# Seven 128-wide block products in place of a two-by-two block product of eight, in a graph network of four layers on one Trainium2 core

## The chip, the core and the metric

The kernel runs on one NeuronCore of a Trainium2 chip. A core has TensorE for matrix products (PE in the profile, with its weight loads in a row of their own, PEld), VectorE (DVE), ScalarE (ACT), GpSimd (POOL) and SyncE (SP), which here only starts DMA transfers. The metric is the device time of one execution in microseconds. Before the change it is 1382.38 us, the median of three runs (1381.41 to 1382.77).

## What is computed

The input `x` has 64 batches of 256 nodes with 128 features, all in fp32, and one 256x256 matrix `adj`, called A here, is shared by all batches. Four layers follow each other, and each ends with a residual sum and a layer norm (LN). Cut to what matters:

```python
def _layernorm(x, axis=-1, eps=1e-5):
    m = jnp.mean(x, axis=axis, keepdims=True)
    v = jnp.var(x, axis=axis, keepdims=True)
    return (x - m) / jnp.sqrt(v + eps)
# layer 0: powers of A up to the third
parts = [x_1[..., None], _chebyshev(adj0, x_1, CONV_ORDER), _chebyshev(adj1, x_1, CONV_ORDER)]
y_1 = jnp.einsum('bnik,iok->bno', jnp.concatenate(parts, axis=3), weight_1)
# layer 1
output = jnp.einsum('nm,bmo->bno', adj, jnp.einsum('bnf,fo->bno', x, weight)) + bias
# layer 2, A_norm = d (A + I) d
out = jnp.einsum('bnc,oc->bno', jnp.einsum('nm,bmc->bnc', A_norm, x), W) + b
# layer 3: five steps of a gated unit, both matrices are A
m_in = jnp.einsum('nm,bmd->bnd', in_matrix, h)
u3 = h @ u3_w.T + u3_b
z = jax.nn.sigmoid(av @ w3_w.T + w3_b + u3)
r = jax.nn.sigmoid(av @ w4_w.T + w4_b + u3)
hv = jnp.tanh(av @ w5_w.T + w5_b + (r * h @ u5_w.T + u5_b))
h = (1.0 - z) * h + z * hv
```

Every one of the 64 batches is therefore multiplied by A, by A squared or by the normalised A eight times in the form that the kernel uses: once in layer 0 (with A squared; the rest of layer 0 is folded into products with the weights and one more product with A), once in layer 1, once in layer 2 and five times in layer 3.

## The kernel before

**Tiling.** The batches are taken in groups of two (`NB`), so that a group's activations fill one tile of 128 partitions by 512 fp32 numbers: two batches times two halves of the nodes times 128 features. There are 31 groups of two and, because `ONES` is (0, 2), two groups of one batch at the end. A product with A (`propagate`, L457) takes each batch's two halves of the nodes as stationary operands of 128x128 and streams the 256 columns of A's transpose past each, four matmuls per group into one PSUM bank, and ScalarE copies the bank to SBUF (`copied`, L417). Each matmul instruction of the program appears twice in the trace[...]: counts of matmuls in the profile are twice those of the program.

**What else a group does.** Layer 0 has 8 matmuls of 256 columns with the weights and 4 of 256 columns with A; layers 1 and 2 have 4 matmuls each of 128 columns with the weights; each step of layer 3 has five matmuls of 512 columns (`product`, L517) in transposed form, three activations on ScalarE (`gate_`, L520: r, z, hv) and four elementwise operations on VectorE (`tensor`, L527: rh, d, e, hT), and then a transpose of 32x32 blocks on VectorE and a way through DRAM that brings h back with the nodes on the partitions (`packed`, L500). The last step of a group goes back through DRAM too (`turned`, `brought`), or, for the last `END` batches, through TensorE.

**LN.** `statistics` (L422) takes four `bn_stats` and four `bn_aggr` on VectorE, adds the epsilon there, and raises to the power of -1/2 on GpSimd (`rs`). `normalise` (L446) then subtracts the mean and multiplies by `rs` on VectorE, in four instructions of 128 columns. In layers 1 and 2 GpSimd also adds the bias to the residual (`yb`, L595).

**The order of the work.** Nothing is left to a scheduler at run time. Each operation is entered in a `Plan` (L50) with its engine, a cost in ns, a lag until others can see its result and a rank. `Plan.order` (L80) then plays the program through: of all operations whose inputs are there it takes the one that can start first, and among those that can start together the one of the lowest rank, that is of the oldest group.

```python
                    key = (max(at, t0), op.rank, op.seq)
                    if pick is None or key < pick[0]:
                        pick = (key, op)
```

The operations are issued in the order of their planned starts, and each engine runs its own in that order. The plan's costs are `pe_cost`, `dve_cost` and `act_cost` (L141 to L149) or numbers written at the call. The plan also gives out buffers: eight PSUM banks, 54 tiles of the kind `w`, and so on (`slots`, L199).

**Groups in flight.** A group may begin only when the group `ACTIVE` places before it has finished (`gate`, L649 to L653), so at most six groups are under way. The last `LEVEL` groups get nearly equal ranks, which lets them advance side by side to the end.

Of the kernel before, what the change touches and what calls it, by code (L numbers as in the profile page):

```python
# [13 lines left out]
P = 128  # L14
NB = 2
ACTIVE = 6
HEAD = 4
LEVEL = 6
END = 8
STEPS = 5  # L20
WARM = 12
ONES = (0, 2)
# [4 lines left out]
class Val:  # L27
# [3 lines left out]
    def __init__(self, kind, shape, name, nb=NB):  # L31
        self.kind, self.shape, self.name, self.nb = kind, shape, name, nb
        self.writer, self.readers, self.users = None, [], []
        self.slot = self.tile = None
# [15 lines left out]
class Plan:  # L50
# [9 lines left out]
    def add(self, engine, cost, lag, rank, run, reads=(), writes=(), after=()):  # L60
        if engine == "SP":
            lag += 700
        op = Op(len(self.ops), rank, engine, cost, lag, run, [*reads, *writes])
        op.deps.update(after)
        for v in reads:
            op.deps.add(v.writer)
            v.readers.append(op)
        for v in writes:
            if v.writer is not None:
                op.deps.add(v.writer)  # L70
            op.deps.update(v.readers)
            v.writer, v.readers = op, []
# [72 lines left out]
def dve_cost(elements):  # L145
    return elements / 0.96 + 75
# [7 lines left out]
def kernel(  # L154
# [42 lines left out]
    SHAPES = {"bank": [P, 512], "x": [P, 512], "w": [P, 512], "st": [P, Q * 6], "mv": [P, Q * 2],  # L197
              "ve": [P, Q], "rs": [P, Q]}
    slots = {"bank": BANKS, "x": ACTIVE + 3, "w": 54, "dram1": 8, "dram2": 16, "st": 8, "mv": 8, "ve": 8, "rs": 8}  # L199
# [15 lines left out]
    def load(rank, name, shape, src):  # L215
        v = constant(name, shape)
# [13 lines left out]
    def warmed():  # L230
        for i in range(WARM):
# [5 lines left out]
    a_nat = load(-9, "a_nat", [P, T, N], adj.rearrange("(t p) m -> p t m", p=P))  # L237
# [12 lines left out]
    pre(-8, "PE", 4 * 110, lambda: turn(p_at, a_nat), [a_nat], [p_at])  # L250
# [42 lines left out]
    ahat, anT = constant("ahat", [P, T, N]), constant("anT", [P, T, N])  # L293
# [24 lines left out]


    w1s = load(1.3, "w1s", [P, C], w1)  # L320
    b1s = load(1.4, "b1s", [P, C], bass.AP(tensor=b1.tensor, offset=b1.offset, ap=[[0, P], [1, C]]))
    raw = {name: load(1.5, f"raw_{name}", [P, src.shape[1]], src)
           for name, src in (("w2", w2), ("w4", w4_w), ("w3", w3_w), ("w5", w5_w), ("u3", u3_w), ("u5", u5_w))}
    b2s = load(1.5, "b2s", [P, C], bass.AP(tensor=b2.tensor, offset=b2.offset, ap=[[0, P], [1, C]]))
    both = {name: constant(f"both_{name}", [P, C]) for name in ("w4", "w3", "w5", "w34")}
# [41 lines left out]
    def tile_of(v, q):  # L367
        return nat(v)[:, q, :]

    def pair_of(v, q):  # L370
        return v.ap.rearrange("p (b c t) -> p b t c", c=C, t=T)[:, q // T, q % T, :]
# [8 lines left out]
    class Group:  # L380
# [15 lines left out]
        def rank(self):  # L396
            g = self.start / NB
            return g if g < G - LEVEL else G - LEVEL + (g - G + LEVEL) / 10 + self.count / 100

        def add(self, engine, cost, lag, run, reads=(), writes=()):  # L400
            after = () if self.first else self.gate
            self.count += 1
            op = plan.add(engine, cost, lag, self.rank(), run, reads, writes, after)
# [296 lines left out]
```

## Time and profile before

The page of the profile says of one execution:

| | busy, us | share of 1380.7 us | instructions |
|---|---|---|---|
| PE | 1366.5 | 99% | 5044 |
| PE weight loads | 922.5 | 67% | 5044 |
| DVE | 970.5 | 70% | 2735 |
| ACT | 513.1 | 37% | 833 |
| POOL | 236.1 | 17% | 205 |

Busy time is the time in which an engine had at least one instruction under way. A matmul's duration is longer than its distance to the next one[...]; so a matmul's price is read from the distance between starts in the timeline, not from the mean duration in a group. In a line of the groups, the numbers are: the line of the source, the engine, the operation, what is written and what is read, the shape, the count, the busy time in us, the mean duration of one in ns, and the idle time of the engine just before them. A line of the timeline has the start in us, the length of the (merged) piece in us, then the same names.

### The profile page before, as it was taken

To read this page: it belongs to the slowest core of one execution; us is meant where nothing else is said; L and a number is where in the kernel's file an instruction comes from. 1 tells how busy PE (TensorE), PEld (TensorE's weight loads), DVE (VectorE), ACT (ScalarE), POOL (GpSimd) and SP (SyncE) were. 2 spreads that over 40 slices of the span, in tenths; PEclk is the share of its full clock that TensorE was granted. 3 is DMA by queue.
4 is the path that set the end of the run, shared out by engine and by line. 5 is a ranking of instruction groups with operands and counts; after the bars stand their busy time and mean duration, and the time that the engine had idled before them with its cause. 6 is when DMAs were issued, how large, how long until landed. Compare 5 with 4: busy or idle time off the path is not lost.

```text
span 1380.7 us, 16602 instructions
## 1 busy us (share of the span) xinstructions
PE 1366.5 (99%) x5044; PEld 922.5 (67%) x5044; DVE 970.5 (70%) x2735; ACT 513.1 (37%) x833; POOL 236.1 (17%) x205
## 2 busy tenths in 40 slices
PE   9999999999999999999999999999999999999996
PEld 8866666666667766566676666667666677766664
DVE  4755686867667767776686767668685778875577
ACT  2233433333433233433424333442334332334443
POOL 1400021202111211011121211012221113210001
PEclk9999999999999999999999999999999999999999
DMA  6023233333333332343241334333232432233332
GB/s 177 31 77 91 85 115 115 91 98 105 112 107 90 109 92 75 97 137 110 64 137 54 108 108 117 95 92 106 78 107 84 118 97 85 85 92 90 86 103 65
DMA packets 271112, 134.08 MB, mean 97 GB/s; under 512 B 177584, under 2 KB 243632, under 8 KB 271024
## 3 DMA queue, kind: packets, MB, share of 16 engines
q1 hardware_dynamic: 271024, 133.03, 33.2%
q8 instruction: 40, 0.66, 0.2%
q14 instruction: 48, 0.39, 0.1%
HBM read 67.05 MB, written 65.54 MB: 96 GB/s over the span
## 4 chain that ended last, share of the span: by engine, by line
PE 97%; DVE 2%; DMA 0%; ACT 0%; issue 0%; POOL 0%; SPq 0%; POOLq 0%; DVEq 0%
PE pr L195 30%; PE ph L195 19%; PE pmg L195 19%; PE py L195 16%; PE pm L195 8%; PE pmq L195 4%; DVE y L451 1%; DMA h<-dh 0%; DVE st L427 0%; PE p_a L195 0%; PE warm L232 0%; DVE s L443 0%; DVE d L529 0%; DVE mv L431 0%; DVE e L529 0%
## 5 line engine op out<-in xcount | busy, mean ns | idle before, releaser
L195 PE MATMUL pr<-mg,w435u5T 128*128 128x512 f32 (+1 forms) x660 | 323.3, 580 | 1.7 <-ACT mg L419 1.4
L438 POOL TENSOR_TENSOR rs<-ve,half 128x4 f32<-128x4 f32 (+1 forms) x132 | 137.9, 1049 | 1049.8 <-DVE ve L432 1049.7
L529 DVE TENSOR_TENSOR d<-hv,hT 128x512 f32<-128x512 f32 (+1 forms) x165 | 113.6, 690 | 189.6 <-ACT hv L522 189.2
L195 PE MATMUL pmg<-aTp,h 128*128 128x256 f32 x1024 | 241.7, 379 | 0.4 <-DMA h<-dh 0.4
L195 PEld LDWEIGHTS pmg<-aTp,h 128*128 128x128 f32 x1024 | 200.4, 196 | 50.5 <-issue 24.4
L529 DVE TENSOR_TENSOR rh<-r,hT 128x512 f32<-128x512 f32 (+1 forms) x165 | 116.5, 706 | 128.2 <-ACT r L522 126.9
L195 PEld LDWEIGHTS pr<-mg,w435u5T 128*128 128x128 f32 x660 | 123.6, 190 | 101.0 <-issue 90.4
L419 ACT COPY mg<-pmg 128x512 f32<-128x512 f32 (+1 forms) x165 | 94.6, 573 | 257.0 <-PE pmg L195 236.5
L451 DVE TENSOR_SCALAR y<-s,mv,rs 128x128 f32<-128x128 f32 x512 | 149.7, 357 | 34.0 <-POOL rs L438 32.5
L195 PE MATMUL pr<-hT,w2u3T 128*128 128x512 f32 (+1 forms) x330 | 163.1, 580 | 1.1 <-DVE hT L529 1.1
L522 ACT ACTIVATE z<-pr,bsum 128x512 f32<-128x512 f32 (+1 forms) x165 | 111.3, 674 | 142.2 <-PE pr L195 137.4
L195 PE MATMUL ph<-mg,w435u5T 128*128 128x512 f32 (+1 forms) x330 | 163.4, 579 | 0.0
L195 PE MATMUL ph<-rh,w435u5T 128*128 128x512 f32 (+1 forms) x330 | 163.0, 579 | 0.0
L522 ACT ACTIVATE r<-pr,bsum 128x512 f32<-128x512 f32 (+1 forms) x165 | 111.3, 674 | 135.2 <-PE pr L195 132.7
L522 ACT ACTIVATE hv<-ph,bsum 128x512 f32<-128x512 f32 (+1 forms) x165 | 111.3, 674 | 53.0 <-PE ph L195 50.9
L529 DVE TENSOR_TENSOR e<-z,d 128x512 f32<-128x512 f32 (+1 forms) x165 | 113.8, 691 | 2.5
L529 DVE TENSOR_TENSOR hT<-hT,e 128x512 f32<-128x512 f32 (+1 forms) x165 | 113.1, 687 | 2.5
L427 DVE BATCH_NORM_STATS2 st<-s 128x6 f32<-128x128 f32 x512 | 109.7, 277 | 0.8
L195 PEld LDWEIGHTS ph<-rh,w435u5T 128*128 128x128 f32 x330 | 62.4, 190 | 69.3 <-issue 59.5
L195 PEld LDWEIGHTS ph<-mg,w435u5T 128*128 128x128 f32 x330 | 62.4, 190 | 67.5 <-issue 54.8
L504 DVE STREAM_TRANSPOSE th<-hT 128x512 f32<-128x512 f32 x132 | 91.0, 689 | 2.0
L195 PEld LDWEIGHTS pr<-hT,w2u3T 128*128 128x128 f32 x330 | 61.6, 190 | 42.0 <-issue 25.2
(79 smaller groups left out, 1373.7 us busy)
## 6 DMA issues: line engine op xcount, KB each, us to landing
dh<-th SPq DMA_DIRECT2D x155, 256.0 KB, 2.0
h<-dh SPq DMA_DIRECT2D x256, 128.0 KB, 2.5
x<-in_x_dram SPq DMA_DIRECT2D x31, 256.0 KB, 3.3
hT<-dh SPq DMA_DIRECT2D x124, 64.0 KB, 2.0
out_dram<-y SPq DMA_DIRECT2D x31, 256.0 KB, 2.4
xT<-dx SPq DMA_DIRECT2D x60, 128.0 KB, 2.5
dx<-tx SPq DMA_DIRECT2D x29, 256.0 KB, 2.6
dn<-tn SPq DMA_DIRECT2D x28, 256.0 KB, 2.0
```

The source lines that it names most:

```text
L195: nc.tensor.matmul(o, lhsT, rhs, start=start, stop=stop, skip_group_check=shared)
L419: self.act(lambda: nc.scalar.copy(t.ap, ps.ap), [ps], [t])
L427: nc.vector.bn_stats(st.ap[:, q * 6:(q + 1) * 6], nat(s)[:, q, :])
L438: lambda: nc.gpsimd.tensor_tensor(rs.ap, ve.ap, half[:, :self.q], op=OP.pow), [ve], [rs])
L451: nc.vector.tensor_scalar(nat(y)[:, q, :], nat(s)[:, q, :], mv.ap[:, 2 * q:2 * q + 1], rs.ap[:, q:q + 1], op0=OP.subtract, op1=OP.mult)
L504: self.dve(lambda: nc.vector.transpose(turn.ap.rearrange("p (u j t) -> p u t j", t=T, j=32), src.ap.rearrange("p (u t i) -> p u t i", t=T, ...
L522: self.act(lambda: nc.scalar.activation(t.ap, ps.ap, func, bias=bias[1], scale=1.0), [ps, bias[0]], [t], act_cost(self.width) + 100)
L529: self.dve(lambda: nc.vector.tensor_tensor(out(t), way(a), way(b), op=op), [a, b], [t])
```

## The change

The matrix A is cut into four blocks of 128x128, and the activations of a group into two batches and two halves of nodes. That is a product of two-by-two blocks, which takes eight block products; the change uses a scheme of the Strassen and Winograd kind that needs seven, at the price of sums and differences of blocks before and after. For groups of two batches `propagate` now hands over to a new method, `seven`:

- The sums of A's blocks are made once at the start (`block_sums`), for A, A squared, the normalised A and a row-permuted A.
- The differences of the activations' blocks are made on GpSimd, in three instructions per product with A: `ts01` (256 columns), `ts2` and `ts3` (128 columns each).
- The seven products have 128 columns each and come in four pieces: `first` (one product), `middle` (three), `more` (one) and `rest` (two). All four write one PSUM bank. ScalarE saves the result of `first` before `more` adds to it (`kept`).
- The sums afterwards are four instructions on VectorE (`post11`, `post12`, `post13` of 128 columns and `post2` of 256) and one copy of 128 columns on ScalarE. They take the place of the copy of 512 columns on ScalarE. `rest` has to wait for `post13` and for that copy[...].

The other parts: the last step of LN moves from VectorE to ScalarE (`activation` with scale and bias per partition), for which VectorE negates the mean and GpSimd multiplies it by `rs`; the copies of layer 0's sums out of PSUM move from VectorE to ScalarE; at most eight groups are in flight instead of six, with more buffers of several kinds; there are 32 groups of two batches and none of one; `LEVEL` is 5 instead of 6 and the ranks of the last groups rise faster; the plan's cost of a VectorE operation is raised by 6%, and the new operations have costs written at the call; a few more transposes are made at the start[...]. Some tiles of the preparation are now given out by the plan and reused. The first two groups keep the old four matmuls in layer 0.

```diff
@@ -13,13 +13,13 @@
-ACTIVE = 6
+ACTIVE = 8
 HEAD = 4
-LEVEL = 6
+LEVEL = 5
 END = 8
 STEPS = 5
-WARM = 12
-ONES = (0, 2)
+WARM = 14
+ONES = (0, 0)
...
-    def add(self, engine, cost, lag, rank, run, reads=(), writes=(), after=()):
+    def add(self, engine, cost, lag, rank, run, reads=(), writes=(), after=(), joint=False):
+
         if engine == "SP":
             lag += 700
-        op = Op(len(self.ops), rank, engine, cost, lag, run, [*reads, *writes])
+        op = Op(len(self.ops), rank, engine, cost, lag, run, list(dict.fromkeys([*reads, *writes])))
         op.deps.update(after)
         for v in reads:
-            op.deps.add(v.writer)
+            op.deps.update(v.writers)
             v.readers.append(op)
         for v in writes:
-            if v.writer is not None:
-                op.deps.add(v.writer)
             op.deps.update(v.readers)
-            v.writer, v.readers = op, []
+            if not joint:
+                op.deps.update(v.writers)
+                v.writers = []
+            v.writers.append(op)
+            v.readers = []
...
 def dve_cost(elements):
-    return elements / 0.96 + 75
+    return (elements / 0.96 + 75) * 1.06
...
-    SHAPES = {"bank": [P, 512], "x": [P, 512], "w": [P, 512], "st": [P, Q * 6], "mv": [P, Q * 2],
+    SHAPES = {"bank": [P, 512], "x": [P, 512], "w": [P, 512], "th": [P, 384], "q": [P, P], "st": [P, Q * 6], "mv": [P, Q * 2],
               "ve": [P, Q], "rs": [P, Q]}
-    slots = {"bank": BANKS, "x": ACTIVE + 3, "w": 54, "dram1": 8, "dram2": 16, "st": 8, "mv": 8, "ve": 8, "rs": 8}
+    slots = {"bank": BANKS, "x": ACTIVE + 3, "w": 60, "th": 8, "q": 8, "dram1": 8, "dram2": 16, "st": 12, "mv": 12, "ve": 24, "rs": 12}
...
+    def turned_early():
+        turn(p_at, a_nat)
+        warming(4)
+
+    pre(-8, "PE", 8 * 110, turned_early, [a_nat], [p_at, warm])
...
+    sums_of = {}
+
+    def block_sums(rank, name, aTs):
+        v = constant(f"s_{name}", [P, 5, P])
+        a11, a12, a21, a22 = (aTs.ap[:, kt, t * P:(t + 1) * P] for t in range(T) for kt in range(T))
+
+        def run():
+            nc.vector.tensor_add(v.ap[:, 0, :], a21, a22)
+            nc.vector.tensor_sub(v.ap[:, 1, :], v.ap[:, 0, :], a11)
+            nc.vector.tensor_sub(v.ap[:, 2, :], a11, a21)
+            nc.vector.tensor_sub(v.ap[:, 3, :], a12, v.ap[:, 1, :])
+            nc.vector.tensor_scalar(v.ap[:, 4, :], a22, -1.0, None, op0=OP.mult)
+
+        pre(rank, "DVE", 1200, run, [aTs], [v])
+        sums_of[aTs] = v
+
+    block_sums(0.6, "aT", aT)
+    block_sums(0.6, "a2T", a2T)
+    block_sums(0.6, "anT", anT)
+    block_sums(0.7, "aTp", aTp)
...
-            return g if g < G - LEVEL else G - LEVEL + (g - G + LEVEL) / 10 + self.count / 100
+            return g if g < G - LEVEL else G - LEVEL + (g - G + LEVEL) / 10 + self.count / 50
...
-            st, mv, ve, rs = (self.val(k, k + tag) for k in ("st", "mv", "ve", "rs"))
+            st, mv, ve, rs, nm = (self.val(k, n + tag) for k, n in (
+                ("st", "st"), ("mv", "mv"), ("ve", "ve"), ("rs", "rs"), ("ve", "nm")))
 
             def stats():
                 for q in range(self.q):
...
             def aggr():
                 for q in range(self.q):
                     nc.vector.bn_aggr(mv.ap[:, 2 * q:2 * q + 2], st.ap[:, q * 6:(q + 1) * 6])
-                nc.vector.tensor_scalar(ve.ap, mv.ap.rearrange("p (q k) -> p q k", k=2)[:, :, 1], EPS,
-                                        None, op0=OP.add)
+                mean, var = (mv.ap.rearrange("p (q k) -> p k q", k=2)[:, k] for k in range(2))
+                nc.vector.tensor_scalar(ve.ap, var, EPS, None, op0=OP.add)
+                nc.vector.tensor_scalar(nm.ap, mean, -1.0, None, op0=OP.mult)
+
+            def scales():
+                nc.gpsimd.tensor_tensor(rs.ap, ve.ap, half[:, :self.q], op=OP.pow)
+                nc.gpsimd.tensor_tensor(mv.ap[:, :self.q], nm.ap, rs.ap, op=OP.mult)
 
             self.dve(stats, [s], [st], 195 * self.q)
-            self.dve(aggr, [st], [mv, ve], 67 * self.q + 142)
-            self.add("POOL", 1010, 100,
-                     lambda: nc.gpsimd.tensor_tensor(rs.ap, ve.ap, half[:, :self.q], op=OP.pow), [ve], [rs])
+            self.dve(aggr, [st], [mv, ve, nm], 67 * self.q + 240)
+            self.add("POOL", 1420, 100, scales, [ve, nm], [rs, mv])
             return mv, rs
 
...
-                    nc.vector.tensor_scalar(nat(y)[:, q, :], nat(s)[:, q, :], mv.ap[:, 2 * q:2 * q + 1],
-                                            rs.ap[:, q:q + 1], op0=OP.subtract, op1=OP.mult)
-
-            self.dve(run, [s, mv, rs], [y], 257 * self.q)
+                    nc.scalar.activation(nat(y)[:, q, :], nat(s)[:, q, :], AF.Identity, bias=mv.ap[:, q:q + 1],
+                                         scale=rs.ap[:, q:q + 1])
+
+            self.act(run, [s, mv, rs], [y], 400 * self.q)
             return y
 
-        def propagate(self, tag, h, aTs, ins=None, outs=None):
-
-            ps = self.val("bank", "pm" + tag)
+        def propagate(self, tag, h, aTs, ins=None, blocks=False, fast=True):
+
+            if fast and self.nb == 2:
+                return self.seven(tag, h, aTs, ins or tiles, blocks)
+            ps, outs = self.val("bank", "pm" + tag), by_block if blocks else None
...
+        def seven(self, tag, h, aTs, ins, blocks):
+            sums = sums_of[aTs]
+            ps, m = self.val("bank", "pm" + tag), self.val("w", "m" + tag)
+            ts, tq, u = self.val("th", "ts" + tag), self.val("q", "tq" + tag), self.val("th", "us" + tag)
+            w = self.val("q", "ws" + tag)
+            def row(v, k):
+                return v.ap[:, k * P:(k + 1) * P]
+            def o(v, q, blocks=blocks):
+                if v.kind == "q":
+                    return v.ap.rearrange("p (k i) -> p k i", k=4)
+                if blocks:
+                    return v.ap.rearrange("p (k q i) -> p q k i", k=4, i=32)[:, q]
+                return v.ap.rearrange("p (q k i) -> p q k i", k=4, i=32)[:, q]
+            def ts01():
+                nc.gpsimd.tensor_tensor(ts.ap[:, :2 * P].rearrange("p (x c) -> p x c", x=2), ins(h)[:, 1], ins(h)[:, :, 0],
+                                        op=OP.subtract)
+            def ts2():
+                nc.gpsimd.tensor_tensor(row(ts, 2), ins(h)[:, 1, 1], row(ts, 0), op=OP.subtract)
+            def ts3():
+                nc.gpsimd.tensor_tensor(tq.ap, row(ts, 2), ins(h)[:, 0, 1], op=OP.subtract)
+            def block(q, w, a, start=False):
+                mm(row(ps, q), w, a, start, True, shared=True)
+            def first():
+                block(0, ins(h)[:, 0, 0], aTs.ap[:, 0, :P], True)
+            def middle():
+                block(2, row(ts, 0), sums.ap[:, 0, :])
+                block(1, row(ts, 1), sums.ap[:, 2, :])
+                block(3, row(ts, 2), sums.ap[:, 1, :])
+            def more():
+                block(0, ins(h)[:, 0, 1], aTs.ap[:, 1, :P])
+            def rest():
+                block(2, ins(h)[:, 1, 1], sums.ap[:, 3, :])
+                block(1, tq.ap, sums.ap[:, 4, :])
+            def post11():
+                nc.vector.tensor_tensor(row(u, 0), row(u, 1), row(ps, 3), op=OP.add)
+            def post12():
+                nc.vector.tensor_tensor(row(w, 0), row(u, 0), row(ps, 1), op=OP.add)
+            def post13():
+                nc.vector.tensor_tensor(o(m, 3), o(w, 0, False), o(ps, 2, False), op=OP.add)
+            def post2():
+                both = o(u, 0, False)[:, None].to_broadcast([P, 2, 4, 32])
+                nc.vector.tensor_tensor(o(m, slice(1, 3)), o(ps, slice(1, 3), False), both, op=OP.add)
+            started = self.pe(pe_cost(P, 1), first, [h, aTs], [ps])
+            kept = self.act(lambda: nc.scalar.copy(row(u, 1), row(ps, 0)), [ps], [u], act_cost(P))
+            self.add("POOL", 830, 100, ts01, [h], [ts])
+            self.add("POOL", 610, 100, ts2, [h, ts], [ts])
+            self.add("POOL", 590, 100, ts3, [h, ts], [tq])
+            self.pe(pe_cost(P, 3), middle, [ts, sums], [ps], True, (started,))
+            self.pe(pe_cost(P, 1), more, [h, aTs], [ps], True, (kept,))
+            self.dve(post11, [ps, u], [u], 215)
+            self.dve(post12, [ps, u], [w], 215)
+            self.dve(post13, [ps, w], [m], 215)
+            self.act(lambda: nc.scalar.copy(o(m, 0), o(ps, 0, False)), [ps], [m], act_cost(P), True)
+            self.pe(pe_cost(P, 2), rest, [h, tq, sums], [ps], True)
+            self.dve(post2, [ps, u], [m], 340, True)
+            return m
...
-            qT = self.propagate("q", x_, a2T)
+            qT = self.propagate("q", x_, a2T, fast=not near)
...
-                    nc.vector.tensor_copy(nat(s0).rearrange("p (b t) c -> p t b c", t=T)[:, t],
+                    nc.scalar.copy(nat(s0).rearrange("p (b t) c -> p t b c", t=T)[:, t],
                                           four(p)[:, :, 0, :])
 
                 self.pe(pe_cost(self.nb * C, T), second, [v, aT], [py[t]])
-                self.dve(summed, [py[t]], [s0], dve_cost(self.nb * C))
+                self.act(summed, [py[t]], [s0], act_cost(self.nb * C))
...
-                m = self.propagate(f"g{s}", h, ats, ins, by_block)
+                m = self.propagate(f"g{s}", h, ats, ins, True)
...
-                    h, ats, ins = self.packed(f"h{s}", hT), aTp, pair_of
+                    h, ats, ins = self.packed(f"h{s}", hT), aTp, pairs
```

## The prediction

> **What bounds the kernel now.** I read the engines' shares first, then the chain that ended last, then TensorE's waits, then stretches of the span, and last the timeline, for the prices. Page, parts 1 and 4:
>
> ```profile
> PE 1366.5 (99%) x5044; PEld 922.5 (67%) x5044; DVE 970.5 (70%) x2735; ACT 513.1 (37%) x833; POOL 236.1 (17%) x205
> PE 97%; DVE 2%; DMA 0%; ACT 0%; issue 0%; POOL 0%; SPq 0%; POOLq 0%; DVEq 0%
> ```
>
> The chain stays on TensorE. Who TensorE waited for (us in all, times, longest):
>
> ```profile
> PE pth L475 <- DVE hT L529: 2.6, 1, 2.6
> PE pr L195 <- ACT mg L419: 1.4, 3, 0.5
> ```
>
> The whole list comes to 7.6 us. Engines by stretch (us; busy PE, PEld, DVE, ACT, POOL; clock; DMA):
>
> ```profile
> 700.00:1000.00 300.00, 300.00 (x1106) 202.22 (x1105) 209.27 (x588) 110.43 (x176) 52.61 (x44) 1.00 0.34 98
> 1350.00:1360.00 10.00, 8.96 (x40) 6.73 (x39) 9.16 (x30) 3.93 (x8) 1.05 (x1) 1.00 0.38 106
> 1360.00:1370.00 10.00, 8.83 (x32) 4.96 (x30) 6.42 (x20) 4.70 (x9) 0.41 (x1) 1.00 0.19 53
> 1370.00:1381.00 11.00, 1.76 (x8) 1.05 (x8) 6.03 (x25) 0.95 (x2) 2.07 (x3) 0.75 0.16 48
> ```
>
> TensorE has no gap in the middle. Its idle time is 1380.7 - 1366.5 = 14.2 us: 2.0 in the first ten us, 1.0 in the middle, 11.2 after 1350. So the kernel's time is the sum of its matmuls and two ends. Prices of matmuls from TensorE's timeline (start, length, ...):
>
> ```profile
> 45.48 1.89 PE L195 MATMUL pm<-anT,y 128*128 128x256 f32 x8
> 47.21 1.05 PE L195 MATMUL py<-w1s,m 128*128 128x128 f32 x8
> 48.10 0.60 PE L195 MATMUL py<-w0p,xT 128*128 128x256 f32 x2
> ```
>
> From start to start, eight entries of 256 columns take 47.21 - 45.48 = 1.73 us and eight of 128 take 0.89. Longer runs give 0.2156 and 0.111 us per entry, and 0.429 for 512 columns. Check: between 100 and 1200 us the groups by shape have 1286, 2309 and 432 entries of 512, 256 and 128 columns, so 552 + 498 + 48 = 1098 us of 1100.
>
> [...]
>
> ```profile
> 709.88 0.68 DVE L529 TENSOR_TENSOR rh<-r,hT 128x512 f32<-128x512 f32 x1
> 710.04 1.65 POOL L595 TENSOR_TENSOR yb<-y,b2s 128x512 f32<-128x512 f32 x1 [1.23 <-DVE y L451]
> 710.59 1.65 DVE L529 TENSOR_TENSOR d<-hv,hT 128x512 f32<-128x512 f32 x1
> ```
>
> yb takes 1.27 us alone and d 0.69; in each other's way both took 1.65. [...]the page of before has one load in all, with sigmoid, tanh and copy mixed[...].
>
> **The change part by part.** TensorE: a product with A goes from 8 x 0.2156 = 1.725 us to 14 x 0.111 = 1.554, so 0.171 saved (the plain ratio 7/8 would give 0.216; the dearer 128-column entry takes a fifth of it). There are 32 x 8 - 2 = 254 such products: 43.4 us off the engine that sets the end. A group costs 25 x 0.859 + (8 + 4) x 0.431 + 8 x 0.222 + 8 x 1.554 = 40.9 us of TensorE, against 42.2.
>
> VectorE, per group. It loses y (4 x 1.1 us) and the copies s0 (2 x 0.41), and gains per product with A three additions of 128 and one of 256 columns with PSUM. Nearest rows: the copies of 128 and 256 columns out of PSUM, 0.285 and 0.412 us long; queued behind each other some 0.08 less. That is 0.99 to 1.27 us, eight times 7.9 to 10.1. With 0.17 for each of four negations, 30.3 (970.5/32) becomes 34 to 36 us of 40.9: 82 to 88%.
>
> GpSimd, per group: yb has 1.27 us at 512 columns and 0.727 at its shortest at 256, so ts01 0.73 and ts2, ts3 0.45 each by the same slope; the plan's own numbers (0.83, 0.61, 0.59) are the upper bound. Eight times 1.63 to 2.03, plus four times 1.02 for the power and 0.2 to 0.4 for the new multiply, plus two yb: 20.5 to 24.5 us. It goes from 17% to 50-60%.
>
> [...]VectorE's d, e, hT, rh (20 x 0.69) and the last residual (0.68) are 14.5 us with two SBUF inputs; those on PSUM take one. [...]How much is lost I scale from before: means less medians of those four operations in their 512-column form sum to about 93 ns, x 155 = 14.4 us lost, at 213 us of undisturbed GpSimd time. At 656 to 784 us that is 44 to 53, 1.4 to 1.7 us per group. VectorE stays at 36 to 38 of 40.9.
>
> ScalarE: y in 16 instructions per group[...]; s0 0.75; 16 copies of 128 columns at 0.266 for eight of 512 at 0.587: 4.3 for 4.7. 16.0 becomes about 22 us. Hidden under TensorE's 40.9, as are the copies moved, the preparation's reuse of tiles and the four block sums (some 6 us of VectorE early, where it is half idle).
>
> Added waits. A product now enters TensorE four times, behind GpSimd (ts), ScalarE (kept) and VectorE (three additions in a row). Alone it takes about ts01 + ts2 1.2, middle and more 0.9, three additions 1.1, rest 0.5, post2 0.5 and the hops, 5 us and more against 2.7. Queued behind a waiting matmul is all of TensorE's later work, so only the order saves it. In the order of the changed kernel, near its middle, pmg of group 28 has 1.9 us of other matmuls between first and middle and 3.2 between more and rest. But VectorE has d and e, 1.4 us[...], among the additions that rest waits for, some 2.8 us together: 0.4 us to spare. One blocked d (up to 1.65) would show. Eight groups instead of six give the room back: some 150 us of chain per group undisturbed (128 before) in 8 x 40.9 = 327 us (6 x 42.2 = 253), a slack of 2.2 times against 2.0. I put the stalls at 8 us (0 to 30): 0.03 us per product.
>
> Ends. After the last product: hv, d, e, hT 2.8 us, transpose 0.6, s, statistics and epsilon 2.3, GpSimd 1.4, y 1.4, output 2.8 and hops 1: 12.5 against the 11.2 idle now; the last groups advance in turn with 5 x 5.8 us of TensorE per step for a chain of about 19, so no more gaps. At the start six more transposes and longer chains of the first groups: +1.5.
>
> Sum: 1382.4 - 43.4 + 1.3 + 1.5 + 8 = 1350.
>
> **The rivals.** (a) The lock makes VectorE the bound: each of the 21 locked operations waits 0.36 us, half of a GpSimd instruction weighted by length, so 35 + 7.6 = 42.6 us per group, x 32 + 15 for the ends = 1378. For it: the three lines above. Against: only 14.4 us lost by 620 operations before. (b) The re-entries stall TensorE: [...]at 0.1 us for each of three re-entries, 254 x 0.3 = 76, so 1342 + 76 = 1418, slower. For it: VectorE near 90%, and 0.4 us to spare where I looked. Against: before, TensorE lost 1 us in the middle though d took up to 1.65. (c) No stalls and cheap ends: 1342.
>
> **How the numbers follow.** My forecast with (c) beside it has 0.75, (a) 0.13, (b) or worse 0.12. A part of (a) ends under the old time. Faster 0.84, same 0.03, slower 0.13. The range goes from no stall with slightly cheaper matmuls, 1335, to (a), 1382; what lies above is (b), with 0.12.
>
> **What would show it.** TensorE's entries of 128 columns 0.111 us apart in runs; TensorE over 97% busy with a total near 1325; VectorE 82 to 93%, GpSimd 50 to 64%, ScalarE about 50%, one table load; d and e longer in the mean by some 0.05 to 0.1 us. TensorE's waits on post11 to post13 and on ts should sum to about 8 us; 40 or more would mean (b), VectorE at 97% (a). I am wrong above all if the waits behind the additions come often, or if separate 128-column entries cost more than those in a run.

## The result, and the profile after

The changed kernel takes 1391.16 us (median of four runs, 1389.97 to 1392.09) against 1382.58 before (1381.41 to 1382.82): a ratio of 1.0063, with a 95% interval of 1.0046 to 1.0081. It is slower by 8.6 us, where the forecast was 1350 and faster, and lies above the range of 1335 to 1382.

Parts 1 and 4 of the page of the changed kernel, busy time by engine and the chain that ended last:

```profile
PE 1347.1 (97%) x6516; PEld 928.3 (67%) x6516; DVE 1114.0 (80%) x3288; ACT 691.1 (50%) x1638; POOL 754.7 (54%) x1089
PE 82%; DVE 13%; issue 2%; ACT 2%; DMA 1%; SPq 1%; DVEq 0%; POOL 0%; ACTq 0%; POOLq 0%
```

Before, the chain was 97% TensorE and 2% VectorE. Now 13% of it is VectorE. TensorE's idle time has gone from 14.2 to 1389.6 - 1347.1 = 42.5 us. Engines by stretch (us; busy PE, PEld, DVE, ACT, POOL; clock; DMA), changed kernel:

```profile
700.00:1000.00 300.00, 295.80 (x1458) 206.16 (x1456) 247.24 (x749) 152.95 (x371) 176.97 (x252) 1.00 0.34 99
1350.00:1360.00 10.00, 10.00 (x40) 5.71 (x40) 6.59 (x16) 4.30 (x9) 3.29 (x6) 1.00 0.37 105
1360.00:1370.00 10.00, 10.00 (x40) 5.67 (x40) 8.91 (x26) 3.86 (x7) 0.00 (x0) 1.00 0.11 29
1370.00:1380.00 10.00, 4.87 (x17) 2.06 (x15) 9.69 (x40) 7.46 (x16) 5.96 (x7) 0.87 0.17 52
1380.00:1390.00 10.00, 1.11 (x4) 0.71 (x4) 2.10 (x12) 3.29 (x8) 1.56 (x4) 0.50 0.26 79
```

The middle, which had no gap, has lost 4.2 us of 300, while no engine is full: VectorE stands at 82% there, GpSimd at 59%. After 1350 TensorE is idle for 13.6 us against the 11.2 before. TensorE's waits in the changed kernel (us in all, times, longest):

```profile
PE pth L591 <- DVE hT L645: 5.2, 2, 4.6
PE pmg L198 <- DVE mg L565: 5.2, 8, 2.1
PE pr L198 <- DVE hT L645: 3.3, 6, 1.2
PE py L198 <- DVE m L569: 2.8, 2, 1.8
PE pm L198 <- DVE m L565: 2.6, 2, 2.2
```

L565 is `post13`, which `rest` waits for, and L569 is `post2`, which the next layer's matmuls wait for. The whole list comes to 33.4 us in 47 waits, against 7.6. It shows only waits longer than the matmul still under way covers, and so does busy time (an entry of 128 columns lasts 0.275 us in the trace, and in a run the next one starts 0.111 us after it): the list grew by 25.8 us and TensorE's idle time by 28.3, while the account below finds 51.8 us lost. TensorE is 97% busy, and yet loses the time that follows.

**The account.** An entry is one record of a matmul in the trace. I took every distance from one entry's start to the next and compared it with the prediction's prices (0.111, 0.2156 and 0.429 us for 128, 256 and 512 columns). Entries more than 20 ns late, from 60 us after the start to 40 us before the last matmul, are called stalls below.

| us, profiled execution | before | after | difference |
|---|---|---|---|
| matmuls at their prices | 1357.7 | 1314.8 | -42.9 |
| entries under 20 ns off, summed | 1.3 | 6.4 | +5.1 |
| stalls (8 and 171 of them) | 2.0 | 44.1 | +42.1 |
| late starts in the first 60 us | 5.0 | 7.9 | +2.9 |
| late starts in the last 40 us | 6.9 | 6.3 | -0.6 |
| after the last matmul's start | 6.5 | 8.8 | +2.3 |
| span | 1380.7 | 1389.6 | +8.9 |

(The rows leave out the first matmul's start, 1.4 us in both, and rounding.) The saving came as reckoned. The stalls ate it. (20 of the 171, of 3.3 us, fall in two stretches of a clock of 0.50, of which the last section tells.)

**One stall in the timeline** of the changed kernel (start, length, engine, ...; what an instruction waited for in brackets):

```profile
510.47 0.61 PE L198 MATMUL pm<-aT,y 128*128 128x128 f32 x4
...
510.91 0.39 PE L198 MATMUL pmq<-s_a2T,x 128*128 128x128 f32 x2
...
511.45 0.47 DVE L559 TENSOR_TENSOR us<-us,pm 128x128 f32<-128x128 f32 x2
...
511.58 0.39 PE L198 MATMUL pmq<-s_a2T,tqq 128*128 128x128 f32 x2
...
511.85 0.97 DVE L645 TENSOR_TENSOR hT<-hT,e 128x512 f32<-128x512 f32 x1
512.23 0.90 POOL L538 TENSOR_TENSOR tqq<-tsq,x 128x128 f32<-128x128 f32 x1
512.73 0.47 DVE L562 TENSOR_TENSOR ws<-us,pm 128x128 f32<-128x128 f32 x2
...
513.13 0.70 DVE L620 STREAM_TRANSPOSE th<-hT 128x512 f32<-128x512 f32 x1
513.76 0.44 DVE L565 TENSOR_TENSOR m<-ws,pm 128x128 f32<-128x128 f32 x2
...
514.15 0.46 PE L198 MATMUL pm<-s_anT,y 128*128 128x128 f32 x2 [2.18 <-DVE m L565]
```

The price of a matmul can be read from the first two lines: four entries of 128 columns in 0.44 us. Then TensorE's next matmul is `rest` of a product of layer 2, and it waits for three additions in a row on VectorE: it writes the blocks that the second and the third read. Two products run side by side, so each addition comes twice. Between them stand another group's `hT`, which takes 0.97 us instead of 0.69 beside GpSimd's `ts3` (0.90 instead of its median of 0.46), and its transpose of 0.70. VectorE runs from 511.45 to 514.20 without a gap. TensorE's next entry starts 2.34 us later than its price would put it, and everything behind `rest` in its queue stands with it. I looked at every late start of over 0.2 us in the same way: there are 54, of 33.0 us together (5 of them, of 1.9 us, at the clock of 0.50), and VectorE is busy in 96% of that time, though it is at 80% overall.

By the matmul that came late (m is the product's result), the 44.1 us are: `rest` 15.4, the matmuls that take a finished product (`pr`, `ph`, `py` from m) 10.6, `pr` from hT 7.9, `ph` from rh 4.3, `middle` 3.1, `first` and `more` 2.6.

### The profile page after: what moved, and what is told of

Same layout as the page of the kernel before. It is cut to its first block, busy times and chain, and to the rows that moved or that the text cites. A ratio compares the mean times of both kernels' runs of the same rounds, so it can differ in the third digit from the quotient of the medians.

```text
span 1389.6 us, 22166 instructions
## 1 busy us (share of the span) xinstructions
PE 1347.1 (97%) x6516; PEld 928.3 (67%) x6516; DVE 1114.0 (80%) x3288; ACT 691.1 (50%) x1638; POOL 754.7 (54%) x1089
## 4 chain that ended last, share of the span: by engine, by line
PE 82%; DVE 13%; issue 2%; ACT 2%; DMA 1%; SPq 1%; DVEq 0%; POOL 0%; ACTq 0%; POOLq 0%
PE pr L198 27%; PE ph L198 18%; PE pmg L198 16%; PE py L198 13%; PE pm L198 6%; PE pmq L198 2%; DVE hT L645 2%; DVE d L645 2%; DVE e L645 2%; DVE st L461 1%; DVE s L481 1%; DMA x<-in_x_dram 1%; DVE rh L645 1%; ACT hv L638 1%; DVE th L620 1%
## 5 line engine op out<-in xcount | busy, mean ns | idle before, releaser
L198 PE MATMUL pr<-mg,w435u5T 128*128 128x512 f32 x640 | 325.0, 597 | 2.3 <-DVE mg L569 2.2
L471 POOL TENSOR_TENSOR rs<-ve,half 128x4 f32<-128x4 f32 x128 | 143.7, 1123 | 232.8 <-DVE nm L468 230.7
L489 ACT ACTIVATE y<-s,mv,rs 128x128 f32<-128x128 f32 x512 | 210.6, 483 | 44.1 <-POOL mv L472 42.7
L645 DVE TENSOR_TENSOR rh<-r,hT 128x512 f32<-128x512 f32 x160 | 125.9, 787 | 53.7 <-ACT r L638 52.8
L198 PE MATMUL pr<-hT,w2u3T 128*128 128x512 f32 x320 | 163.4, 598 | 4.2 <-DVE hT L645 3.3
L645 DVE TENSOR_TENSOR d<-hv,hT 128x512 f32<-128x512 f32 x160 | 122.5, 766 | 55.0 <-ACT hv L638 54.2
L198 PE MATMUL ph<-rh,w435u5T 128*128 128x512 f32 x320 | 163.5, 596 | 2.0 <-DVE rh L645 1.9
L198 PE MATMUL ph<-mg,w435u5T 128*128 128x512 f32 x320 | 163.6, 593 | 0.0
L645 DVE TENSOR_TENSOR hT<-hT,e 128x512 f32<-128x512 f32 x160 | 125.6, 788 | 1.4
L645 DVE TENSOR_TENSOR e<-z,d 128x512 f32<-128x512 f32 x160 | 121.4, 761 | 1.4
```

The lines of the kernel that those rows point to most:

```text
L198: nc.tensor.matmul(o, lhsT, rhs, start=start, stop=stop, skip_group_check=shared)
L471: nc.gpsimd.tensor_tensor(rs.ap, ve.ap, half[:, :self.q], op=OP.pow)
L489: nc.scalar.activation(nat(y)[:, q, :], nat(s)[:, q, :], AF.Identity, bias=mv.ap[:, q:q + 1], scale=rs.ap[:, q:q + 1])
L645: self.dve(lambda: nc.vector.tensor_tensor(out(t), way(a), way(b), op=op), [a, b], [t])
```

## The experiments

Ratios are to the kernel before. "Stalls" are those of the account. In every kernel but e1_no_lock, e2_no_turn and e8_no_post12 nothing of the computation is left out.

| kernel | seven-block products | us | ratio, 95% interval | VectorE | stalls, us |
|---|---|---|---|---|---|
| after | 254 | 1391.16 | 1.0063 (1.0046 to 1.0081) | 80% | 44.1 |
| e4_eight | 0 | 1382.25 | 0.9999 (0.9990 to 1.0007) | 59% | 0.1 |
| e3_layer3 | 160 | 1363.14 | 0.9860 (0.9845 to 0.9874) | 73% | 3.6 |
| e5_layers012 | 94 | 1386.83 | 1.0029 (1.0018 to 1.0040) | 67% | 15.9 |
| e7_no_q | 224 | 1372.31 | 0.9924 (0.9909 to 0.9939) | 79% | 19.2 |
| e11_layers23_order | 192 | 1364.96 | 0.9871 (0.9856 to 0.9885) | 77% | 10.0 |
| e1_no_lock | 254 | 1378.58 | 0.9971 (0.9959 to 0.9982) | 78% | 31.8 |
| e2_no_turn | 254 | 1386.25 | 1.0026 (1.0019 to 1.0033) | 76% | 38.4 |
| e8_no_post12 | 254 | 1382.74 | 1.0002 (0.9994 to 1.0011) | 77% | 35.9 |
| e10_ln_back | 254 | 1433.97 | 1.0366 (1.0350 to 1.0381) | 87% | 82.0 |
| e6_order | 254 | 1376.76 | 0.9955 (0.9941 to 0.9969) | 81% | 28.6 |
| e9_six_groups | 254 | 1457.95 | 1.0541 (1.0523 to 1.0559) | 77% | 101.1 |
| e12_load_only | 0 | 1392.44 | 1.0070 (1.0055 to 1.0085) | 80% | 11.0 |

### Which parts, and which layers

e4_eight takes the seven-block products out and keeps the rest of the change; e3_layer3 keeps them in layer 3 alone; e5_layers012 in layers 0 to 2 alone; e7_no_q in all but layer 0. Each is one condition in `propagate`:

```diff
-            if fast and self.nb == 2:
+            if False:                                                                     # e4_eight
+            if fast and self.nb == 2 and tag[0] == "g":                                   # e3_layer3
+            if fast and self.nb == 2 and (... tag ...) in ('q', '1', '2'):                # e5_layers012
+            if fast and self.nb == 2 and (... tag ...) in ('1', '2', 'g'):                # e7_no_q
```

> The changed kernel with the old four matmuls and one copy for every product, all else of the change kept (LN's last step and layer 0's copies on ScalarE, eight groups in flight, 32 groups of two, the plan's new costs). All theories: no stalls in the middle, TensorE's work as before, 1379 to 1386. If it is above 1388, part of the loss is not of the seven products at all.

> The changed kernel with seven block products only in the five steps of layer 3 (160 products); layers 0 to 2 keep the four matmuls of 256 columns and one copy (94 products). TensorE's work rises by 94 x 0.171 = 16 us. If the stalls go evenly with the products (CHAIN, 50 us over 254 = 0.2 us each, more than the 0.171 saved), 18 us of them go: 1391 + 16 - 18 = 1389. LOCK: GpSimd's 755 us fall to about 560, the stalls in proportion to 37: 1391 + 16 - 13 = 1394. LOAD, with the bunches where layers 0 to 2 with their layer norms meet layer 3: the excess falls to about 15 to 20: 1370 to 1377.

> Seven products in layers 0, 1 and 2 only (94 of the 254); layer 3 keeps its eight. Saved on TensorE: 94 x 0.171 = 16.1 us, so 1366 with no stall at all. Theory OWN (the products of layers 0 to 2 stall TensorE by themselves, because their chains are long: GpSimd, three additions, then LN): they keep most of the some 40 us of excess that the changed kernel has over e3_layer3, so 1395 to 1406, slower than before. Theory BUNCH (VectorE is full for some microseconds only where these products meet the sevens of layer 3, whose additions and locked operations take the room): with 160 products less, VectorE falls to about 66% and the stalls to under 10 us: 1366 to 1376.

> Seven products in layers 1, 2 and 3, eight in layer 0: 224 products, 38.3 us saved on TensorE, 1344 with no stall. If the stalls belong to any product of layers 0 to 2 alike, a third of the 40 us that these layers bring goes: about 1384 (30 x 0.171 = 5 us of saving lost, 13 of stall gone). If VectorE is near a limit that is passed only now and then (BUNCH), 30 products less give more than their share: 1358 to 1372. If layers 1 and 2, with the bias sums of 1.27 us on GpSimd beside them, bring the stalls: 1392 to 1397.

e4_eight is at 1382.25, no difference from before: LN's last step on ScalarE, the copies, eight groups in flight, the raised plan cost and the 32 groups together neither cost nor bring time by themselves. The loss comes only with the seven-block products.

e3_layer3 takes 1363.14, 19.1 us less than e4_eight, and beats both kernels. Parts 1 and 4 of its page:

```profile
PE 1343.6 (99%) x5952; PEld 917.3 (67%) x5952; DVE 996.6 (73%) x2912; ACT 697.6 (51%) x1544; POOL 560.6 (41%) x807
PE 96%; DVE 2%; DMA 1%; SPq 1%; ACT 0%; issue 0%; POOL 0%; ACTq 0%; POOLq 0%; DVEq 0%
```

The chain is on TensorE again. 160 products re-enter TensorE three times each here and stall it for 3.6 us, 0.02 us each. So re-entering does not cost a fixed price per product.

In e5_layers012, 94 products save 16.1 us at the prices and lose 15.9 to stalls, with VectorE at 67%, less than before the change. That is between the two expectations: these products stall by themselves, but for 16 us and not for the 40 they seem to bring to the full change. Here too VectorE is busy in 98% of the stalls' time: its mean of 67% hides that it is full where they lie. The sums are not additive: 3.6 and 15.9 alone, 44.1 together. e7_no_q shows the same from the other side: 30 products of layer 0 less, 5 us of saving lost, and 18.9 us lower, just above what I had given to a limit that is passed only now and then (1358 to 1372).

### The lock

What the prediction calls the lock is seen in the traces as longer times: d took 1.65 us beside `yb` at 710.59 before the change, and 0.69 undisturbed. That one of the engines shuts the other out is not shown. e1_no_lock keeps GpSimd's instructions in their places but has them read almost nothing: each subtraction becomes memsets of about its undisturbed length, the first with a subtraction of four columns. (The products then take constants for their differences.) The second of the three, `ts2`:

```diff
-                nc.gpsimd.tensor_tensor(row(ts, 2), ins(h)[:, 1, 1], row(ts, 0), op=OP.subtract)
+                nc.gpsimd.memset(row(ts, 2), 0.01)
+                nc.gpsimd.memset(row(ts, 2), 0.03)
```

> The changed kernel with the same order on every engine, but GpSimd's three difference instructions per product (ts01, ts2, ts3) replaced: a 4-column subtraction of h, so that the wait for h stays, and memsets that write for about as long (about 0.7, 0.4 and 0.4 us) and read nothing. The differences are not computed, so the products with A are of constants. Theory LOCK (GpSimd's reads hold VectorE's four two-input operations up, 56 us in the changed kernel by their means over 0.69 us, and that is what stalls TensorE): d, e, rh and hT fall back to about 0.70 us, the excess of TensorE's spacing between 60 and 1340 us falls from 50 us to below 15, time 1345 to 1357. Theory LOAD (VectorE's work comes in bunches in which no other TensorE work is left; the lock only adds): the operations fall back too, but the excess stays at 30 or more, time 1370 to 1382. Theory CHAIN (each re-entry of a product waits for its hops, whatever the load): no change, 1387 to 1391.

It took 1378.58, 12.6 us less. Groups by line and form (count, then busy us and mean ns, then idle before), two of the changed kernel and the same two of e1_no_lock:

```profile
L645 DVE TENSOR_TENSOR hT<-hT,e 128x512 f32<-128x512 f32 x160 | 125.6, 788 | 1.4
L645 DVE TENSOR_TENSOR d<-hv,hT 128x512 f32<-128x512 f32 x160 | 122.5, 766 | 55.0 <-ACT hv L638 54.2
L648 DVE TENSOR_TENSOR hT<-hT,e 128x512 f32<-128x512 f32 x160 | 115.4, 724 | 1.4
L648 DVE TENSOR_TENSOR d<-hv,hT 128x512 f32<-128x512 f32 x160 | 112.5, 703 | 63.4 <-ACT hv L641 62.6
```

GpSimd is busy for 630.9 us, against 754.7. Undisturbed (the medians before the change), hT and d take 0.69 us. What single operations among rh, d, e and hT take above 0.69 sums to 58 us in the changed kernel and to 16.5 in e1_no_lock, as before the change. Of the 42 us by which these operations got shorter, 12.6 at most came out as time (GpSimd's steps end sooner as well: `ts2` and `ts3` take 0.41 us instead of 0.59 and 0.58). It is a share of the stalls (44.1 to 31.8), not the whole cause.

### VectorE's load

Three kernels change what VectorE does, in different places. e2_no_turn leaves the 128 transposes of 0.7 us between layer 3's steps out, and the untransposed tile goes to DRAM. e8_no_post12 leaves the second addition of each product out. e10_ln_back puts LN's last step on VectorE again, and takes the negation and the multiply away.

```diff
 # e2_no_turn, in packed
-            self.dve(lambda: nc.vector.transpose(...), [src], [turn])
+            self.dve(lambda: None, [src], [turn])
 # e8_no_post12
-                nc.vector.tensor_tensor(o(m, 3), o(w, 0, False), o(ps, 2, False), op=OP.add)
+                nc.vector.tensor_tensor(o(m, 3), o(u, 0, False), o(ps, 2, False), op=OP.add)
-            self.dve(post12, [ps, u], [w], 215)
+            self.dve(lambda: None, [ps, u], [w], 215)
 # e10_ln_back, in normalise
-                    nc.scalar.activation(nat(y)[:, q, :], nat(s)[:, q, :], AF.Identity, bias=..., scale=...)
+                    nc.vector.tensor_scalar(nat(y)[:, q, :], nat(s)[:, q, :], mv.ap[:, 2 * q:2 * q + 1],
+                                            rs.ap[:, q:q + 1], op0=OP.subtract, op1=OP.mult)
```

> The changed kernel with the same order, but the 32x32 transpose on VectorE after each of the first four steps of layer 3 left out (128 instructions of 0.70 us, 90 us of VectorE; the way through DRAM then carries the untransposed tile, so the later steps multiply a wrong h). [...]LOAD: VectorE falls from 1114 to about 1025 us busy and TensorE's excess from 50 us to 30 or less, time 1365 to 1375. LOCK: the excess hardly moves, time 1384 to 1391. CHAIN: the chain of a product is not touched, time 1386 to 1391.

> The second of the three additions between the pieces more and rest is left out, in every seven-block product (post13 adds the first sum instead, so the values are not the reference's); everything else keeps its order. That takes 254 x 0.271 = 69 us from VectorE, about as much as e2_no_turn took elsewhere (which gave 5 us), but here from the chain that TensorE's rest waits for. Theory CHAIN (the length of the three additions is what TensorE waits for): 0.27 us less in each of the some 100 to 170 places where it waits, up to 35 us, 1356 to 1366. Theory FULL (VectorE's other work in these stretches is what is in the way): as in e2_no_turn, 5 to 10 us, 1381 to 1386.

> The changed kernel with LN's last step on VectorE, as before the change (GpSimd's multiply and the negation of the mean go too). VectorE gets 512 instructions of about 0.27 us and loses 128 of 0.17, some +115 us, to about 89%; GpSimd and ScalarE lose work. Theory FULL: what VectorE does in its full stretches is paid by TensorE, 0.3 to 0.5 of the added time: 1420 to 1450. Theory RE-ENTRY (only the steps between a product's pieces count, and LN lies outside them): 1388 to 1400.

VectorE's busy time goes from 1114.0 to 1052.8, 1067.8 and 1249.7 us. The time goes down by 4.9 and 8.4 us and up by 42.8: 0.08, 0.18 and 0.32 us per us of VectorE. In the first two the order is that of the changed kernel; in e10_ln_back the plan made a new one, so the 42.8 us hold what that did as well. Shortening the chain that `rest` waits for is worth twice as much per us as work elsewhere, but not the 0.27 us times a hundred waits that a pure latency would give. And LN's last step, outside every product, costs 43 us when it stands in VectorE's queue. What counts is all that is queued on VectorE around the additions, and the curve is steep upwards.

### The order, and the groups in flight

e6_order has the changed kernel's instructions in another order: GpSimd's, ScalarE's and VectorE's operations of a product get a rank 100 lower, so the plan takes them first when they could start at the same time as others. e9_six_groups sets `ACTIVE` back to 6. e11_layers23_order has e6_order's ranks and seven-block products in layers 2 and 3.

```diff
+            self.hot = True    # set in seven, from first to post2; False elsewhere
-            op = plan.add(engine, cost, lag, self.rank(), run, ...)
+            op = plan.add(engine, cost, lag, self.rank() - (100 if self.hot and engine != "PE" else 0), run, ...)
```

> The same instructions as the changed kernel; only the plan's ranks differ: the operations of a product with A that are not TensorE's (differences, kept, additions, corner copy) go ahead of everything else that could start at the same time on their engine. Theory ORDER (TensorE waits because its product's additions stand behind d, e, hT, y-statistics or transposes of other groups in VectorE's queue): the stalls of over 0.2 us, 33 us, fall by more than half, total 1360 to 1372. Theory FULL (VectorE has no room in these stretches; who goes first only decides who waits): stalls of about the same sum in other places, 1384 to 1400.

> The changed kernel with six groups in flight, as before the change, instead of eight. Theory ROOM (the longer chain per group needs groups to hide it; what counts is chain against the time that the groups in flight give): some 150 us of chain in 6 x 41 = 246 us, a slack of 1.6 where before the change it was 2.0, so the stalls grow several times over: 1420 to 1460. Theory FULL (VectorE has its full stretches however many groups are under way): 1385 to 1400.

> Seven products in layers 2 and 3 only (192), with the ranks of e6_order. 32.8 us saved on TensorE: 1349.6 with no stall. Stalls so far grew faster than the number of products (9 us of excess at 160, 26 at 224, 50 at 254); by a line between the first two, 192 products lose 17, less some for the ranks: 1357 to 1364, about as good as e3_layer3 or a little better. If layer 2 stalls at the rate of e5_layers012 (0.18 us per product) and the ranks do nothing: 1364 to 1368.

Order alone is worth 14.4 us: 1376.76, between the two expectations, and the only kernel here that computes all 254 products in full and is faster than before. VectorE does the same work (1113.1 us), and the stalls fall from 44.1 to 28.6, above all those of finished products (10.6 to 3.6). So about a third of the stalls was a matter of who stands behind whom; the ranks of three engines were changed together, so it is not shown that VectorE's order alone did it. The others stayed.

Six groups in flight cost 66.8 us against eight. The stalls of 101.1 us spread over `rest` 25, finished products 25, hT 21, `first` and `more` 15, `middle` 10. That is the expectation of the theory that groups give the room (1420 to 1460). So room matters; that eight gave enough was the error.

e11_layers23_order came to 1364.96, not told apart from e3_layer3 by the intervals: 32 products more bring 5.5 us at the prices and lose 6.4 to stalls.

### The load without the re-entry

The last kernel takes the two halves of the suspicion apart. Eight products everywhere, as in e4_eight, but GpSimd's differences and VectorE's additions are run as well, on the product's operands and bank, into tiles that nobody reads:

```diff
-            return self.copied("m" + tag, ps)
+            m = self.copied("m" + tag, ps)
+            if fast:
+                ... # ts01, ts2, ts3 on GpSimd, as in seven
+                self.dve(lambda: nc.vector.tensor_tensor(row(u, 0), row(m, 0), row(ps, 3), op=OP.add), [ps, m], [u], 215)
+                self.dve(lambda: nc.vector.tensor_tensor(row(w, 0), row(u, 0), row(ps, 1), op=OP.add), [ps, u], [w], 215)
+                self.dve(lambda: nc.vector.tensor_tensor(row(u, 0), row(w, 0), row(ps, 2), op=OP.add), [ps, w], [u], 215)
+                ... # and one of 256 columns, as post2
+            return m
```

> Eight products everywhere, as in e4_eight (1382), but GpSimd's three differences and VectorE's four additions are run all the same, beside the product and into tiles that nobody reads: VectorE and GpSimd get the load of the seven, 80% and 54%, and TensorE never waits for these instructions. The output is the reference's. Theory RE-ENTRY (a full VectorE costs TensorE time only because a seven-block product needs VectorE, ScalarE and GpSimd between its own pieces): 1382 to 1388. Theory FULL (VectorE's load alone, by delaying d, e, hT and LN, starves TensorE): as much excess as in the changed kernel, some 40 us, 1415 to 1430.

Page parts 1 and 4 and the stretch 700 to 1000 us of e12_load_only:

```profile
PE 1368.8 (98%) x4992; PEld 913.0 (66%) x4992; DVE 1118.8 (80%) x3288; ACT 720.7 (52%) x1384; POOL 732.0 (53%) x1089
PE 91%; DVE 5%; issue 1%; ACT 1%; DMA 1%; SPq 1%; POOL 0%; ACTq 0%; POOLq 0%; DVEq 0%
```

```profile
700.00:1000.00 300.00, 299.69 (x1109) 202.29 (x1108) 246.15 (x730) 157.04 (x305) 163.28 (x242) 1.00 0.34 98
```

VectorE, GpSimd and ScalarE are loaded as in the changed kernel (1114.0, 754.7 and 691.1 us), and in the middle TensorE lost 0.3 us of 300 and not 4.2. The time is 1392.44, 10.2 us above e4_eight; the stalls are 11.0 us, 7.8 of them at hT and rh, that is in layer 3's own chain. The expectations were 1382 to 1388 and 1415 to 1430: near the first, but the load is not free. Of the 11.0 us 7.5 come after 1150 us, where the last groups advance side by side; from 60 to 1150 us the load alone costs 3.5 us of stalls, and the changed kernel has 34.3 there.

One difference remains: TensorE's work is longer here, so VectorE has less to do per us of it (1118.8 to 1358 us, 0.82, against 1114.0 to 1315, 0.85). That is not what spares the stalls: e1_no_lock, e2_no_turn and e8_no_post12 have 0.80 or 0.81 and 32 to 38 us of them. The plan's order is another one as well, and no run takes that apart.

The stretches make it plain. Cut the middle into 255 pieces of 5 us. VectorE is at least 95% busy in 46 of them before the change, in 75 after and in 79 in e12_load_only. What TensorE loses in those pieces is 1.3, 27.6 and 10.0 us. VectorE was often full before the change too, and it cost next to nothing. My reading is that TensorE had other groups' matmuls ready and needed VectorE only at hT, rh and LN.

So in the middle: neither load nor re-entry 0.1 us of stalls (e4_eight), the load alone 11.0, both 44.1. The 33 us between the last two need that TensorE itself depends on these steps, and the list by late matmuls tells where: in the middle of a product (`rest` 15.4 us) and at its end (10.6 us at matmuls that take a result which VectorE, and no longer ScalarE, completes). No run separates these two. That the re-entry without the load costs little is shown by layer 3's products only (3.6 us with VectorE at 73%).

## Why the prediction was wrong

**The step that failed** is in "Added waits": "Eight groups instead of six give the room back: some 150 us of chain per group undisturbed (128 before) in 8 x 40.9 = 327 us (6 x 42.2 = 253), a slack of 2.2 times against 2.0. I put the stalls at 8 us (0 to 30): 0.03 us per product." They rose by 42.1 us, 0.17 per product, which is the whole saving per product (0.171). The slack is an average over a group's way, and it does not order the kernels: before, with 2.0, 2.0 us of stalls; after, with 2.2, 44.1. Six groups (1.6 by the same count) gave 101.1, so the room is a real condition. What the average left out is that VectorE is full for some microseconds at a time, and that a product now needs it in the middle and at the end. The prediction had the case in hand: 0.4 us to spare where it looked, and "one blocked d (up to 1.65) would show". It looked at one place, and then let the average overrule it.

**The rivals.** The result is rival (b), "the re-entries stall TensorE", slower, which had 0.12, at some 60% of its size (44 us for 76), and not by its 0.1 us at each re-entry, which was the author's guess and stands in no trace: of 6515 distances 171 are long, and 54 of these hold 33.0 us. Its mark, 40 us or more of stalls, is met in the spacing; the list of waits that the prediction named for it shows only some 15 us on the additions, `ts` and the saved copy. Rival (a), VectorE's longer times beside GpSimd, is worth 12.6 us at most (e1_no_lock), and VectorE is at 80%, not 97%. What spoke against (b), "before, TensorE lost 1 us in the middle though d took up to 1.65", was true and no argument, since before the change no product waited, between its own matmuls, for additions that could stand behind d. Of the prediction's three lines, rh kept its 0.68 us though `yb` began at 710.04, within it; `yb` had 0.52 us beside rh (until 710.56) before d began at 710.59. So its 1.65 us cannot be put down to d alone, as the prediction does.

**Other terms.** TensorE's saving: 42.9 us at the prices (43.4 forecast); but entries of 128 columns are 1.3 ns longer than 0.111 us on the mean, which takes most of the 5.1 us in the table. Additions: 280, 271, 274 and 417 ns, 1.24 us per product, in the range of 0.99 to 1.27. VectorE 34.8 us per group with the longer times in it, 80%, just under the 82 to 93 of the forecast. What single operations among rh, d, e and hT take above 0.69 us: 58 us, above the 44 to 53 of the forecast. GpSimd 23.6 us per group (20.5 to 24.5), ScalarE 21.6 (22). LN's last step on ScalarE: 483 ns for one and 1.65 us for four in a row, 6.6 us per group; the plan's 0.40 for one is right for four in a row. One table load, of 1.28 us, as before the change and as forecast (that it would stay at one was not shown beforehand). Ends: +2.9 at the start (1.5), +1.7 at the tail (1.3). Had the stalls stayed at 8, the sum would have come to some 1357.

**What stays open.** Why a product of layers 0 to 2 stalls at 0.17 us (e5_layers012) and one of layer 3 at 0.02 (e3_layer3), with VectorE less loaded in the first: no run separates their longer way (LN before them, the bias sums of 1.33 us on GpSimd beside them) from how the plan places them. Also open is how much of the 28.6 us that e6_order left a better order could still take, and whether a plan with measured costs in place of those written at the calls would find one: no run changes them.

## What to carry to other kernels

When a change splits a step of the bounding engine into pieces with another engine's work between them, price the waits where the other engine is full for a few microseconds, not from its mean share or from a slack over the whole chain; look at ten such places in the order, not at one. Use the cheaper form only where the other engine has room: here 160 of 254 products gave 19 us, and the other 94 took more than that back. Where the room is, the mean share does not tell (layers 0 to 2 alone stalled with VectorE at 67%); leaving one place out at a time does. When TensorE seems 97% busy, read the distances between starts; busy time and the list of waits hid about half of the loss.

## What the runs showed of the hardware

**The clock fell to half for 3.413 us after two of the four longest stalls.** After a stall of 2.23 us that ended at 325.28, TensorE's stretches of one us in the changed kernel (columns as above) read:

```profile
325.00:326.00 1.00, 0.72 (x6) 0.72 (x7) 1.00 (x7) 0.22 (x1) 0.67 (x2) 1.00 0.07 27
326.00:327.00 1.00, 1.00 (x8) 1.00 (x7) 0.87 (x4) 1.00 (x4) 0.77 (x2) 0.56 0.18 54
327.00:328.00 1.00, 1.00 (x4) 0.62 (x3) 0.76 (x4) 0.57 (x3) 0.88 (x2) 0.50 0.52 147
328.00:329.00 1.00, 1.00 (x3) 0.34 (x2) 0.57 (x1) 0.00 (x0) 0.90 (x2) 0.50 0.21 62
```

The clock is at 0.50 for 3.413 us, from 326.12 on, and entries of 512 columns come 0.85 us apart instead of 0.429. It happens twice in the middle of the changed kernel, at a cost of some 1.7 us each: the second time at 1203.35, again for 3.413 us, after a stall of 1.98 us that ended at 1202.47. After the other two of the four longest stalls, of 2.11 us (to 193.54) and of 2.34 us (to 514.15, shown above), the clock stayed at 1.00. So the length of the last stall alone does not tell whether the clock falls, and what decides it was not shown. Before the change there is no such fall in the middle; at the end of the trace the clock falls in both kernels, at 1375.55 us before and at 1377.43 after.

**Memsets on GpSimd did not lengthen VectorE's operations.** With memsets in place of the differences, GpSimd was still busy for 630.9 us, and rh, d, e and hT took no more above 0.69 us than before the change (16.5 us in both, with GpSimd busy for 236.1 us before).

**After two long stalls the two entries of the late matmul took longer.** Each matmul of the program has two entries in the trace. After the stalls at 514.15 and 325.28, the two entries of 128 columns took 0.29 us (to 514.44) and 0.34 us (to 325.62) instead of 0.222.
